# A ninth convolution tap chosen by image half, in a matmul that skips the padded row

## The chip, the cores and the metric

The kernel runs on one core of a Trainium2 chip. The metric is the device time of one execution in microseconds, as the median of three runs. TensorE (PE) multiplies matrices, and its weight loads (PEld) are listed apart from its matmuls; VectorE (DVE), ScalarE (ACT) and GpSimd (POOL) work element by element; SyncE (SP) issues DMAs, as ACT and POOL do too.

## The reference

Four residual layers work on an input x of shape (4, 32, 32, 16): batch, height, width, channels. Each layer normalises x over 8 groups of channels and adds the result of a convolution-like operator. In the first three layers this operator has its own 3x3 kernel for every one of the 1024 output positions (i, j):

```python
first = jnp.einsum('ijpq,bpqc->bijc', M2, inputs)
K = jnp.transpose(G, (2, 3, 4, 0, 1, 5)).reshape(kh, kw, c, h * w * f)
shifted = lax.conv_general_dilated(inputs, K, window_strides=(1, 1), padding='SAME', ...)
shifted = shifted.reshape(b, h, w, h, w, f)
diff = jax.nn.relu(inputs[:, :, :, None, None, :] - shifted)
second = jnp.einsum('ijpq,bpqijc->bijc', W2, diff)
return first - L * second
```

So for each position (i, j) and each filter the whole image is convolved with 9 taps x 16 channels, the result is subtracted from the normalised image, clipped at zero, and summed over the image with the weights W. The fourth layer is a filter in the frequency domain; the change does not touch it. With 'SAME' padding, a tap of the upper row of the 3x3 kernel reads only zeros where it is applied to the image's first row, and a tap of the lower row reads only zeros at the image's last row.

## The kernel before

**Tiling.** Positions are worked on in 128 blocks of 8 positions x 16 filters, which are the 128 columns of the weights. A block and one of the four batches make a group. Its result, 128 x 1024 pixels, lies in two PSUM banks, one for the upper 16 image rows (`half` 0) and one for the lower 16 (`half` 1). The contraction over 9 taps x 16 channels is 144 deep. It is split into three operands (L539 to L548): `ga` with image 0 (four taps, 64 rows, in fp32), `gb` with image 1 (four taps, 64 rows, in fp32) and `gn` with image 2 (the ninth tap, in fp32r). For the ninth tap, weights and pixels are each cut into a rounded high part and a remainder, which gives four products of 16 channels, so again 64 rows. Partitions 0 to 63 of each image serve the upper half and partitions 64 to 127 the lower half, so the matmuls of the two halves use different rows of the array. An fp32 matmul shows in the trace as two passes, each with its own weight load; the fp32r matmul shows as one. VectorE then takes the minimum with zero, multiplies by the weights W and sums, in one instruction (L550), into `acc`.

**Image layout.** Each of the three images is a tile of 128 partitions x 4 (l) x 2 (batch of the pair) x 4 (cc) x 34 values. An image row is 32 values in a field of 34, and one batch's 16 rows are read with the pattern 4 x 4 x 32. The order of taps is one list for both halves, with tap 8 (lower right) as the ninth:

```python
TAPS = [0, 1, 3, 4, 2, 5, 6, 7, 8]
```

**Order of the work.** The order is written out by hand (`manual_schedule`). A layer (`conv_layer`, L499) begins with the first 8 blocks for batches 0 and 1, then the same blocks for batches 2 and 3, goes on through the blocks 8 to 119 for all four batches, and ends with the last 8 blocks for batches 0 and 1 and then for 2 and 3. Each of these part jobs for one pair has 16 groups. Beside them run small steps: G weights are loaded (`load_g`) and prepared (`prepare_g`: POOL subtracts on `ga`, ACT casts `gn`, VectorE subtracts its remainder), W tiles are loaded by SP (`load_w`), and the term with M (`first_term`, L378) is computed.

**The images of layer 0** come from the host (`raw`), through `load_first` (L183) on SP. `first_images` (L196) normalises them in place: VectorE for images 0 and 2 (`first_tap`, `last_tap`), ACT for most of image 1, and POOL clears the pixels that stand for padding (`clear`, L210). The first matmuls wait for this.

**The images of layers 1 and 2** are rebuilt when a pair of batches has ended its layer, while the other pair's 16 groups run: `store_image` (L340) normalises, cuts into high part and remainder (L345, L347), copies edges (L348 on POOL, L349 on ACT), and stores three kinds of rows (whole, high, remainder) to DRAM. `load_image` (L356) then loads each tap's shifted view with 24 DMAs, dealt in turn to SP, ACT and POOL; loads that need an edge copy come last. SP's loads of W stand behind its share of these.

Of the kernel before, what the change touches and what calls it, by code (L numbers as in the profile page):

```python
# [29 lines left out]
F32 = mybir.dt.float32  # L30
F32R = mybir.dt.float32r
AF = mybir.ActivationFunctionType
ALU = mybir.AluOpType
# [4 lines left out]
P = 128  # L38
B, C, S = 4, 16, 32
NBLK = 128  # L40
TAPS = [0, 1, 3, 4, 2, 5, 6, 7, 8]
ROW = 2 * 4 * 34
RUN = ROW - 2
GC = 8
NK = S // 2
NF = S * NK
# [9 lines left out]
def conv_stack_kernel(ctx, tc, x, raw, M, W, first_w, G, h0, coef, cst, dft, idp, idq, out):  # L56
# [31 lines left out]

    ys, ye, img = [], [], []
    for a in range(2):  # L90
        ys.append(const.tile([P, 3, 2, 4, 34], F32, name=f"y{a}"))
        ye.append(const.tile([P, 3, 2, 4, 34], F32, name=f"e{a}"))
        img.append(dram.tile([10, C, 3, ROW], F32, name=f"img{a}"))
    hd = dram.tile([8 + C * HLEN], F32, name="hd")
    fd = dram.tile([P, B, 2, 2, S], F32, name="fd")
    td = dram.tile([NK, 2, S, 2 * P], F32, name="td")
# [78 lines left out]
    def image_tiles(a):  # L175


        ims[a] = [
            imp.tile([P, 4, 2, 4, 34], d, tag=f"im{a}{k}", name=f"im{a}{k}")
            for k, d in enumerate((F32, F32, F32R))  # L180
        ]

    def load_first(a, which, b=slice(0, 2)):  # L183

        if a not in ims:
            image_tiles(a)
            nine[a] = st.tile([P, 4, 2, 4, 34], F32, name=f"nine{a}")
        to = nine[a] if which == 2 else ims[a][which]
        nc.sync.dma_start(
            out=to[:, :, b].rearrange("p l b cc x -> p l (b cc x)"),  # L190
            in_=raw[:, a, which].rearrange("p (l b n) -> p l b n", l=4, b=2)[:, :, b].rearrange(
                "p l b n -> p l (b n)"
            ),
        )

    def first_images():  # L196
# [13 lines left out]
        def clear(which, a, b=slice(0, 2)):  # L210

            top, bottom = (0, 0, slice(0, S)), (3, 3, slice(0, S))
            left, right = ((slice(0, 4), slice(0, 4), slice(x, x + 1)) for x in (0, S - 1))
            parts = {
                0: [(g, g + 16, left) for g in range(0, P, 32)] + [(0, 32, top)],
                1: [(g, g + 32, right) for g in (0, 64)]
                + [(g + 32, g + 48, left) for g in (0, 64)]
                + [(0, 16, top), (96, P, bottom)],
                2: [(0, P, right), (64, P, bottom)],
            }[which]  # L220
            for lo, hi, (l, cc, x) in parts:
                nc.gpsimd.memset(ims[a][which].bitcast(F32)[lo:hi, l, b, cc, x], 0.0)

        def first_tap(b, which=0):
            v = of(ims[b // 2][which], b)
# [1 line left out]

        def last_tap(b):

            v, v8, m = of(nine[b // 2], b), of(ims[b // 2][2], b), neg[:, b : b + 1]  # L230
# [101 lines left out]
    def make_image(a, xt):  # L332
# [4 lines left out]
        yield  # L337
        load_image(a)

    def store_image(a, xt, neg, rstd):  # L340
        split = lambda t: t.rearrange("p b (cc q) -> p b cc q", q=S)
        whole, hi, lo = (ys[a][:, k, :, :, 1:33] for k in range(3))
        normalise(a, xt, neg, rstd)
        y = yc[a]
        nc.vector.tensor_copy(hi.bitcast(F32R), split(y))  # L345
        nc.scalar.copy(whole, split(y))
        nc.vector.tensor_tensor(lo, split(y), hi, ALU.subtract)  # L347
        nc.gpsimd.tensor_copy(ye[a][96:, :, :, 1:, :], ys[a][96:, :, :, :3, :])  # L348
        nc.scalar.copy(ye[a][:32, :, :, :3, :], ys[a][:32, :, :, 1:, :])  # L349
        flat = lambda t: t.rearrange("p k b cc x -> p (k b cc x)")  # L350
        rows = img[a].rearrange("p c k x -> p c (k x)")
        nc.sync.dma_start(out=rows[1:9].rearrange("p c x -> (p c) x"), in_=flat(ys[a]))
        nc.scalar.dma_start(out=rows[0], in_=flat(ye[a][7 * C :]))
        nc.scalar.dma_start(out=rows[9], in_=flat(ye[a][:C]))

    def load_image(a):  # L356
        image_tiles(a)
        taps = [(n // 4, n % 4, 0, TAPS[n]) for n in range(8)]
        taps += [(2, n, 1 + n % 2, 8) for n in range(4)]
        jobs = [(half, *tap) for tap in taps for half in range(2)]  # L360

        jobs.sort(key=lambda job: job[4] // 3 == 2 * job[0])
        for n, (half, k, slot, which, tap) in enumerate(jobs):
            at, p = 64 * half + C * slot, 4 * half + tap // 3
            (nc.sync, nc.scalar, nc.gpsimd)[n % 3].dma_start(  # L365
                out=ims[a][k][at : at + C]
                .bitcast(F32)
                .rearrange("c l b cc x -> c l (b cc x)")[:, :, :RUN],
                in_=img[a][p : p + 4, :, which, tap % 3 : tap % 3 + RUN].rearrange(
                    "l c x -> c l x"  # L370
                ),
            )

    def load_m(mt, layer, pm):
        nc.sync.dma_start(out=mt, in_=M[layer][:, pm])
# [123 lines left out]
    def conv_layer(layer, xt, finish, side=(), also=iter(())):  # L499


        acc = [work.tile([P, 2, NBLK], F32, tag=f"acc{a}", name=f"acc{a}") for a in range(2)]
        xn = xp.tile([P, B, NBLK], F32, tag="x", name="x")
        result = {}

        def beside():
            result["xr"] = yield from first_term(layer, xt)
            yield from side

        beside = beside()  # L510
        last = range(NBLK - GC, NBLK)
        jobs = [(range(GC), (0, 1)), (range(GC), (2, 3))]
        jobs += [(range(blk, blk + GC), range(B)) for blk in range(GC, NBLK - GC, GC)]
        jobs += [(last, (0, 1)), (last, (2, 3))]
        for job, (blks, batches) in enumerate(jobs):
            pairs = job < 2, job >= len(jobs) - 2
            groups = [[blk] for blk in blks]
            if layer == job == 0:

                groups[:2] = [[0, 1]]  # L520
            for group in groups:
                for blk in group:
                    k = blk - blks[0]
                    if any(pairs):

                        if k in ((4, 6) if job != len(jobs) - 2 else (0, 2)):
                            list(load_w())
                    elif k % 2 == 0:
                        list(load_w())
                    if k == (3 if job == 0 else 1):  # L530
                        list(load_g(layer, blk // GC + 1))
                    if job and k == 6:
                        list(prepare_g(layer, blk // GC + 1))
                    if job == len(jobs) - 2:
                        next(also, None)
                for b, blk in ((b, blk) for b in batches for blk in group):
                    wt = wts[64 * layer + blk // 2][:, blk % 2, :]
                    pt = pair_psum()
                    for n, (w, im) in enumerate(zip(gt[layer, blk // GC], ims[b // 2])):  # L539
                        for half in range(2):  # L540
                            rows = slice(64 * half, 64 * half + 64)
                            nc.tensor.matmul(  # L542
                                pt[:, half, :],
                                lhsT=w[rows, blk % GC, :],
                                rhs=im[rows, :, b % 2, :, :S],
                                start=n == 0,
                                stop=n == 2,
                            )  # L548
                    junk = junkp.tile([P, S * S], F32, tag="junk", name="junk")
                    nc.vector.scalar_tensor_tensor(  # L550
                        junk,
                        pt.rearrange("p h m -> p (h m)"),
                        0.0,
                        wt,
                        ALU.min,
                        ALU.mult,
                        accum_out=acc[b // 2][:, b % 2, blk : blk + 1],
                    )
# [525 lines left out]
```

## Time and profile before

The kernel takes 3104.75 us, median of 3 runs (3104.68 to 3104.94). The profile is of one execution:

| | |
|---|---|
| span of the profiled execution | 3103.0 us |
| TensorE clock granted | 1.000 |
| TensorE busy | 3094.0 us, 16268 matmuls |
| weight loads busy | 1618.2 us |
| VectorE busy | 2066.7 us |
| POOL busy | 239.6 us |
| ScalarE busy | 74.2 us |
| DMA | 322.46 MB, mean 104 GB/s |
| `ga`, `gb`, `gn` matmul records of L542 | 6144, 6144, 3072; mean 590, 588, 805 ns |
| VectorE L550 | 1536 of mean 1224 ns |

Matmuls are pipelined: the duration of a record is its time from the queue to its last result, and records overlap. The pace of TensorE is read from the distance between starts. "Issue" as a releaser means that nothing in the profile shows what was waited for.

### The profile page before, as it was taken

To read this page: it belongs to the slowest core of one execution; us is meant where nothing else is said; L and a number is where in the kernel's file an instruction comes from. 1 tells how busy PE (TensorE), PEld (TensorE's weight loads), DVE (VectorE), ACT (ScalarE), POOL (GpSimd) and SP (SyncE) were. 2 spreads that over 40 slices of the span, in tenths; PEclk is the share of its full clock that TensorE was granted. 3 is DMA by queue.
4 is the path that set the end of the run, shared out by engine and by line. 5 is a ranking of instruction groups with operands and counts; after the bars stand their busy time and mean duration, and the time that the engine had idled before them with its cause. 6 is when DMAs were issued, how large, how long until landed. Compare 5 with 4: busy or idle time off the path is not lost.

```text
span 3103.0 us, 39162 instructions
## 1 busy us (share of the span) xinstructions
PE 3094.0 (100%) x16268; PEld 1618.2 (52%) x16268; DVE 2066.7 (67%) x3358; ACT 74.2 (2%) x93; POOL 239.6 (8%) x279
## 2 busy tenths in 40 slices
PE   9999999999999999999999999999999999999999
PEld 7854555555555554544545454555444545445454
DVE  7667666666667765666666666776666666666664
ACT  1000000000000000000000000000000000000000
POOL 1022220000000101000000000010100000000000
PEclk9999999999999999999999999999999999999999
DMA  7353443333332745333333333274644454445422
GB/s 231 102 146 89 108 115 95 89 89 95 102 89 62 158 129 129 89 89 95 102 89 89 95 102 89 62 152 128 144 100 97 100 113 104 97 95 119 95 44 42
DMA packets 71003, 322.46 MB, mean 104 GB/s; under 512 B 10409, under 2 KB 20393, under 8 KB 45481
## 3 DMA queue, kind: packets, MB, share of 16 engines
q1 hardware_dynamic: 60592, 302.24, 39.2%
q10 hardware_dynamic: 6152, 9.99, 1.8%
q0 software_dynamic: 4080, 7.72, 1.2%
q8 instruction: 127, 2.08, 0.3%
q14 instruction: 52, 0.42, 0.1%
HBM read 313.64 MB, written 6.28 MB: 103 GB/s over the span
## 4 chain that ended last, share of the span: by engine, by line
PE 100%; DMA 0%; DVE 0%; issue 0%; ACTq 0%; DVEq 0%; ACT 0%
PE pt L542 97%; PE pt L822 1%; PE pt L402 1%; PE pt L576 0%; DMA ga<-in_G_dram 0%; PE pt L649 0%; DVE junk L550 0%; PE pt L690 0%; PE pt L248 0%; DVE ga L460 0%; PE pt L121 0%; ACTq L81 0%; DVE xo L959 0%; DVE d L150 0%; DVE d L153 0%
## 5 line engine op out<-in xcount | busy, mean ns | idle before, releaser
L550 DVE SCALAR_TENSOR_TENSOR junk<-pt,w 128x1024 f32<-128x1024 f32 x1536 | 1880.6, 1224 | 989.0 <-PE pt L542 971.7
L542 PE MATMUL pt<-im,ga 64*128 64x512 f32 x6144 | 1607.4, 590 | 0.0
L542 PE MATMUL pt<-im,gb 64*128 64x512 f32 x6144 | 1600.6, 588 | 0.0
L542 PE MATMUL pt<-im,gn 64*128 64x512 f32 x3072 | 1276.0, 805 | 0.0
L542 PEld LDWEIGHTS pt<-im,gb 64*128 64x128 f32 x6144 | 636.7, 185 | 682.6 <-issue 672.4
L542 PEld LDWEIGHTS pt<-im,ga 64*128 64x128 f32 x6144 | 626.4, 187 | 409.2 <-DVE junk L550 278.3
L542 PEld LDWEIGHTS pt<-im,gn 64*128 64x128 f32 x3072 | 319.7, 186 | 340.3 <-issue 328.5
L460 POOL TENSOR_TENSOR ga<-ga,cs 128x1024 f32<-128x1024 f32 (+1 forms) x48 | 112.5, 2345 | 2025.8 <-DMA ga<-in_G_dram 2025.0
L550 DVE DVE_READ_ACCUMULATOR junk<-pt,w 128x1 f32 x1536 | 127.6, 83 | 0.0
L468 DVE TENSOR_TENSOR gn<-g,gn 32x1024 fp32r<-32x1024 f32 (+2 forms) x98 | 117.7, 1201 | 2.7 <-ACT gn L464 0.6
L464 ACT CAST gn<-g 128x1024 fp32r<-128x1024 f32 (+2 forms) x49 | 50.4, 1029 | 2256.5 <-PE pt L542 2088.2
L417 POOL DMA_DIRECT2D fd<-ft x48 | 25.3, 533 | 318.2 <-ACT ft L409 307.5
L822 PE MATMUL pt<-t,y 128*32 128x512 f32 (+3 forms) x352 | 23.9, 432 | 0.0
L705 POOL COPY hs<-v 32x512 f32<-32x512 f32 x16 | 17.1, 1072 | 47.2 <-ACT v L699 46.6
L946 DVE TENSOR_TENSOR xo<-xo,both 128x512 f32<-128x512 f32 x2 | 1.4, 692 | 26.7 <-DMA both<-sd 26.7
L822 PEld LDWEIGHTS pt<-t,y 128*32 128x32 f32 x352 | 10.9, 110 | 12.8 <-issue 10.9
L365 POOL DMA_DIRECT2D im<-img x32 | 16.1, 513 | 9.3 <-PE pt L542 6.6
L620 POOL TENSOR_TENSOR H<-H,d 128x256 f32<-128x256 f32 x8 | 6.8, 850 | 93.2 <-DVE d L625 92.9
L822 PE MATMUL pt<-t,yp 128*32 128x512 f32 (+3 forms) x192 | 13.6, 434 | 0.0
L348 POOL COPY e<-y 32x612 f32<-32x612 f32 x4 | 2.8, 692 | 129.4 <-DVE y L347 129.4
L402 PE MATMUL pt<-mt,yt 128*64 128x512 f32 x48 | 11.0, 599 | 0.0
L402 PE MATMUL pt<-w,yt 128*64 128x512 f32 x48 | 10.8, 592 | 0.0
(107 smaller groups left out, 192.5 us busy)
## 6 DMA issues: line engine op xcount, KB each, us to landing
w<-in_W_dram SPq DMA_DIRECT2D x188, 1024.0 KB, 7.5
g<-in_G_dram SPq DMA_DIRECT2D x47, 512.0 KB, 7.8
ga<-in_G_dram SPq DMA_DIRECT2D x47, 512.0 KB, 3.5
gb<-in_G_dram SPq DMA_DIRECT2D x47, 512.0 KB, 5.4
mt<-in_M_dram SPq DMA_DIRECT2D x12, 512.0 KB, 9.6
w<-in_M_dram SPq DMA_DIRECT2D x12, 512.0 KB, 4.1
t<-hd ACTq DMA_DIRECT2D x28, 160.0 KB, 7.8
t<-hd SPq DMA_DIRECT2D x28, 160.0 KB, 8.8
```

The costliest lines, as they stand in the source:

```text
L348: nc.gpsimd.tensor_copy(ye[a][96:, :, :, 1:, :], ys[a][96:, :, :, :3, :])
L365: (nc.sync, nc.scalar, nc.gpsimd)[n % 3].dma_start(out=ims[a][k][at : at + C] .bitcast(F32) .rearrange("c l b cc x -> c l (b cc x)")[:, :, ...
L402: nc.tensor.matmul(pf[64 * h : 64 * h + 64], lhsT=yt[:, k].rearrange("k b c -> k (b c)"), rhs=mt[:, bass.ts(h, 512)], start=(k == 0), stop ...
L417: nc.gpsimd.dma_start(out=fv[h, cc, b], in_=ft[at : at + C, cc])
L460: engine.tensor_tensor(gv, gv, mid.unsqueeze(1).to_broadcast([P, gv.shape[1], C]), ALU.subtract)
L464: nc.scalar.copy(gn, g9)
L468: nc.vector.tensor_tensor(lo, g9[r : r + 32], lo.bitcast(F32), ALU.subtract)
L542: nc.tensor.matmul(pt[:, half, :], lhsT=w[rows, blk % GC, :], rhs=im[rows, :, b % 2, :, :S], start=n == 0, stop=n == 2,)
L550: nc.vector.scalar_tensor_tensor(junk, pt.rearrange("p h m -> p (h m)"), 0.0, wt, ALU.min, ALU.mult, accum_out=acc[b // 2][:, b % 2, blk : ...
L620: mul = lambda o, u, w: nc.gpsimd.tensor_tensor(o, u, w, ALU.mult)
L705: nc.gpsimd.tensor_copy(hs[quarter[u], :, bass.ts(c, 8)], v[quarter[c], bass.ts(u, 8)].rearrange("q p m -> q m p"),)
L822: nc.tensor.matmul(rows.rearrange("n (j r) -> n j r", j=C)[:, :, 8 * cc :], lhsT=y(cc).rearrange("p q b -> p (q b)"), rhs=ts[k][q][:, :, : ...
```

## The change

The ninth tap is now chosen by image half. For the upper half it is tap 2 (upper right), for the lower half tap 8 (lower right); tap 8 takes the place of tap 2 among the other eight taps of the upper half. So in each half the ninth tap reads only padding in one image row: the first row in the upper half, the last row in the lower half. Its matmul leaves this row out, and so has 480 columns in place of 512. Image 2 is laid out anew: 2 (batch) x 4 (l) x 4 (cc) x 32, so that one batch's 16 rows are one run of 512 values. In DRAM the high parts and the remainders are stored in the same packed form, shifted by one pixel (both ninth taps look one pixel to the right), and a load of image 2 becomes two DMAs, one for each batch of the pair. The host arranges `raw` and the weights G to match.

```diff
-TAPS = [0, 1, 3, 4, 2, 5, 6, 7, 8]
+TAPS = [0, 1, 3, 4, 8, 5, 6, 7, 2], [0, 1, 3, 4, 2, 5, 6, 7, 8]
+NINE = 2 * 4 * 32
...
-            imp.tile([P, 4, 2, 4, 34], d, tag=f"im{a}{k}", name=f"im{a}{k}")
-            for k, d in enumerate((F32, F32, F32R))
+            imp.tile([P, *shape], d, tag=f"im{a}{k}", name=f"im{a}{k}")
+            for k, (d, shape) in enumerate(
+                ((F32, (4, 2, 4, 34)), (F32, (4, 2, 4, 34)), (F32R, (2, 4, 4, S)))
+            )
...
+        if which == 2:
+            nc.sync.dma_start(
+                out=nine[a][:, b].rearrange("p b l cc x -> p (b l cc x)"),
+                in_=src[:, b.start * 2 * NINE : b.stop * 2 * NINE],
+            )
+            return
...
-                + [(0, 16, top), (96, P, bottom)],
-                2: [(0, P, right), (64, P, bottom)],
+                + [(96, P, bottom)],
+                2: [(0, P, right)],
...
-        nc.vector.tensor_copy(hi.bitcast(F32R), split(y))
-        nc.scalar.copy(whole, split(y))
-        nc.vector.tensor_tensor(lo, split(y), hi, ALU.subtract)
-        nc.gpsimd.tensor_copy(ye[a][96:, :, :, 1:, :], ys[a][96:, :, :, :3, :])
-        nc.scalar.copy(ye[a][:32, :, :, :3, :], ys[a][:32, :, :, 1:, :])
+        hi, lo = hi[..., : S - 1], lo[..., : S - 1]
+        nc.vector.tensor_copy(hi.bitcast(F32R), y[..., 1:])
+        nc.scalar.copy(whole[..., 1:33], y)
+        nc.vector.tensor_tensor(lo, y[..., 1:], hi, ALU.subtract)
+        for e, v in zip(in_rows(ye[a]), in_rows(ys[a])):
+            nc.gpsimd.tensor_copy(e[96:, :, 1:, :], v[96:, :, :3, :])
+            nc.scalar.copy(e[:32, :, :3, :], v[:32, :, 1:, :])
...
-        taps = [(n // 4, n % 4, 0, TAPS[n]) for n in range(8)]
+        taps = [(n // 4, n % 4, 0, n) for n in range(8)]
         taps += [(2, n, 1 + n % 2, 8) for n in range(4)]
-        jobs = [(half, *tap) for tap in taps for half in range(2)]
+        jobs = [(half, *tap, TAPS[half][n]) for *tap, n in taps for half in range(2)]
...
+            if which:
+                moves = [
+                    (to[:, b].rearrange("c l cc x -> c l (cc x)"), src[:, :, bass.ts(b, NINE // 2)])
+                    for b in range(2)
+                ]
+            else:
+                moves = [(to.rearrange("c l b cc x -> c l (b cc x)")[:, :, :size], src)]
+            for out, src in moves:
+                (nc.sync, nc.scalar, nc.gpsimd)[n % 3].dma_start(
+                    out=out, in_=src.rearrange("l c x -> c l x")
+                )
...
+                            px = (slice(S, None), slice(0, -S))[half] if n == 2 else slice(None)
+                            if n == 2:
+                                rhs = im[rows, b % 2].rearrange("p l cc x -> p (l cc x)")[:, px]
+                            else:
+                                rhs = im[rows, :, b % 2, :, :S]
                             nc.tensor.matmul(
-                                pt[:, half, :],
+                                pt[:, half, px],
                                 lhsT=w[rows, blk % GC, :],
-                                rhs=im[rows, :, b % 2, :, :S],
+                                rhs=rhs,
                                 start=n == 0,
                                 stop=n == 2,
                             )
...
-        taps = g[:, P:], g[:, :64], g[:, 64:P]
-        arrays[f"G{i}"] = np.stack([np.tile(t, (1, P // t.shape[1], 1)) for t in taps], 1)
+        parts = slice(8 * C, None), slice(0, 4 * C), slice(4 * C, 8 * C)
+        taps = [[np.tile(t[:, part], (1, 1 if n else 4, 1)) for t in g] for n, part in enumerate(parts)]
+        arrays[f"G{i}"] = np.stack([np.concatenate(t, 1) for t in taps], 1)
```

More of the change, by code (lines that the diff above doesn't have):

```diff
@@ L90, in conv_stack_kernel @@
     for a in range(2):
-        ys.append(const.tile([P, 3, 2, 4, 34], F32, name=f"y{a}"))
-        ye.append(const.tile([P, 3, 2, 4, 34], F32, name=f"e{a}"))
-        img.append(dram.tile([10, C, 3, ROW], F32, name=f"img{a}"))
+        ys.append(const.tile([P, ROW + 2 * NINE], F32, name=f"y{a}"))
+        ye.append(const.tile([P, ROW + 2 * NINE], F32, name=f"e{a}"))
+        img.append(dram.tile([10, C, ROW + 2 * NINE], F32, name=f"img{a}"))
     hd = dram.tile([8 + C * HLEN], F32, name="hd")
@@ L186, in load_first @@
             image_tiles(a)
-            nine[a] = st.tile([P, 4, 2, 4, 34], F32, name=f"nine{a}")
-        to = nine[a] if which == 2 else ims[a][which]
+            nine[a] = st.tile([P, 2, 4, 4, S], F32, name=f"nine{a}")
+        src = raw[:, a, 4 * ROW * which :][:, : 4 * (NINE if which == 2 else ROW)]
+        if which == 2:
[4 more added lines that the diff above has]
+            return
+        to = ims[a][which]
         nc.sync.dma_start(
             out=to[:, :, b].rearrange("p l b cc x -> p l (b cc x)"),
-            in_=raw[:, a, which].rearrange("p (l b n) -> p l b n", l=4, b=2)[:, :, b].rearrange(
+            in_=src.rearrange("p (l b n) -> p l b n", l=4, b=2)[:, :, b].rearrange(
                 "p l b n -> p l (b n)"
@@ L212, in clear @@
             top, bottom = (0, 0, slice(0, S)), (3, 3, slice(0, S))
+            t = ims[a][which].bitcast(F32)
+            if which == 2:
+                t = t.rearrange("p b l cc x -> p l b cc x")
             left, right = ((slice(0, 4), slice(0, 4), slice(x, x + 1)) for x in (0, S - 1))
@@ L217, in clear @@
                 + [(g + 32, g + 48, left) for g in (0, 64)]
-                + [(0, 16, top), (96, P, bottom)],
-                2: [(0, P, right), (64, P, bottom)],
+                + [(96, P, bottom)],
+                2: [(0, P, right)],
             }[which]
             for lo, hi, (l, cc, x) in parts:
-                nc.gpsimd.memset(ims[a][which].bitcast(F32)[lo:hi, l, b, cc, x], 0.0)
+                nc.gpsimd.memset(t[lo:hi, l, b, cc, x], 0.0)
         def first_tap(b, which=0):
@@ L228, in last_tap @@
         def last_tap(b):
-            v, v8, m = of(nine[b // 2], b), of(ims[b // 2][2], b), neg[:, b : b + 1]
+            v, v8 = (
+                t[:, b % 2].rearrange("p l cc x -> p (l cc x)") for t in (nine[b // 2], ims[b // 2][2])
+            )
+            m = neg[:, b : b + 1]
             nc.vector.tensor_scalar(v8, v, m, rstd[:, b : b + 1], ALU.add, ALU.mult)
@@ L338, in make_image, with in_kinds, in_rows @@
         load_image(a)
+    def in_kinds(t):
+        whole = t[:, :ROW].rearrange("p (b cc x) -> p b cc x", b=2, cc=4)
+        pieces = t[:, ROW:].rearrange("p (k b cc x) -> p k b cc x", k=2, b=2, cc=4)
+        return whole, pieces[:, 0], pieces[:, 1]
+    def in_rows(t):
+        return (
+            t[:, :ROW].rearrange("p (b cc x) -> p b cc x", b=2, cc=4),
+            t[:, ROW:].rearrange("p (kb cc x) -> p kb cc x", kb=4, cc=4),
+        )
     def store_image(a, xt, neg, rstd):
-        split = lambda t: t.rearrange("p b (cc q) -> p b cc q", q=S)
@@ L342, in store_image @@
-        whole, hi, lo = (ys[a][:, k, :, :, 1:33] for k in range(3))
         normalise(a, xt, neg, rstd)
-        y = yc[a]
-        nc.vector.tensor_copy(hi.bitcast(F32R), split(y))
-        nc.scalar.copy(whole, split(y))
-        nc.vector.tensor_tensor(lo, split(y), hi, ALU.subtract)
-        nc.gpsimd.tensor_copy(ye[a][96:, :, :, 1:, :], ys[a][96:, :, :, :3, :])
-        nc.scalar.copy(ye[a][:32, :, :, :3, :], ys[a][:32, :, :, 1:, :])
-        flat = lambda t: t.rearrange("p k b cc x -> p (k b cc x)")
@@ L351, in store_image @@
[L351 to L354, printed above, removed]
+        y = yc[a].rearrange("p b (cc q) -> p b cc q", q=S)
+        whole, hi, lo = in_kinds(ys[a])
+        hi, lo = hi[..., : S - 1], lo[..., : S - 1]
+        nc.vector.tensor_copy(hi.bitcast(F32R), y[..., 1:])
+        nc.scalar.copy(whole[..., 1:33], y)
@@ L356, in load_image @@
+        nc.vector.tensor_tensor(lo, y[..., 1:], hi, ALU.subtract)
+        for e, v in zip(in_rows(ye[a]), in_rows(ys[a])):
+            nc.gpsimd.tensor_copy(e[96:, :, 1:, :], v[96:, :, :3, :])
+            nc.scalar.copy(e[:32, :, :3, :], v[:32, :, 1:, :])
+        rows = img[a]
+        nc.sync.dma_start(out=rows[1:9].rearrange("p c x -> (p c) x"), in_=ys[a])
+        nc.scalar.dma_start(out=rows[0], in_=ye[a][7 * C :])
+        nc.scalar.dma_start(out=rows[9], in_=ye[a][:C])
     def load_image(a):
@@ L364, in load_image @@
             at, p = 64 * half + C * slot, 4 * half + tap // 3
[L365 to L372, printed above, removed]
+            start, size = (ROW + NINE * (which - 1), NINE) if which else (tap % 3, RUN)
+            src = img[a][p : p + 4, :, start : start + size]
+            to = ims[a][k][at : at + C].bitcast(F32)
+            if which:
[8 more added lines that the diff above has]
+                    out=out, in_=src.rearrange("l c x -> c l x")
+                )
     def load_m(mt, layer, pm):
@@ L1029 @@
     raw = np.zeros((2, 4, C, 2, 3, 4, 2, 4, 34), x.dtype)
-    for n in range(12):
-        dy, dx = divmod(TAPS[min(n, 8)], 3)
-        v = around[:, dy : dy + S, dx : dx + S].reshape(2, 2, 4, 2, 4, S, C)
-        raw[:, n % 4, :, :, n // 4, :, :, :, :S] = v.transpose(3, 6, 0, 4, 1, 2, 5)
+    for half in range(2):
+        for n in range(12):
+            dy, dx = divmod(TAPS[half][min(n, 8)], 3)
+            v = around[:, dy : dy + S, dx : dx + S].reshape(2, 2, 4, 2, 4, S, C)[:, :, :, half]
+            raw[half, n % 4, :, :, n // 4, :, :, :, :S] = v.transpose(5, 0, 3, 1, 2, 4)
+    raw = raw.reshape(P, 2, 3, 4, 2, 4, 34)
+    raw = [raw[:, :, 0], raw[:, :, 1], raw[:, :, 2, ..., :S].transpose(0, 1, 3, 2, 4, 5)]
+    raw = np.concatenate([v.reshape(P, 2, -1) for v in raw], 2)
     arrays = {
         "x": x.reshape(B, 4, 8, S, C).transpose(2, 4, 0, 1, 3).reshape(P, B, NBLK),
-        "raw": raw.reshape(P, 2, 3, -1),
+        "raw": raw,
     }
@@ L1050 @@
             arrays["first_w"] = np.repeat(w.reshape(64, 8, 2 * S * S)[:4], C, axis=1)
-        g = g[:, :, :, TAPS].transpose(0, 2, 3, 4, 1, 5).reshape(NBLK // GC, GC, 9 * C, P)
-        g = g.transpose(0, 2, 1, 3).reshape(NBLK // GC, 9 * C, GC * P)
-        taps = g[:, P:], g[:, :64], g[:, 64:P]
-        arrays[f"G{i}"] = np.stack([np.tile(t, (1, P // t.shape[1], 1)) for t in taps], 1)
+        g = [
+            g[:, :, :, taps].transpose(0, 2, 3, 4, 1, 5).reshape(NBLK // GC, GC, 9 * C, P)
+            for taps in TAPS
+        ]
+        g = [t.transpose(0, 2, 1, 3).reshape(NBLK // GC, 9 * C, GC * P) for t in g]
+        parts = slice(8 * C, None), slice(0, 4 * C), slice(4 * C, 8 * C)
+        taps = [[np.tile(t[:, part], (1, 1 if n else 4, 1)) for t in g] for n, part in enumerate(parts)]
+        arrays[f"G{i}"] = np.stack([np.concatenate(t, 1) for t in taps], 1)
     pairs = lambda t: t.reshape(-1, 4, 4, C).transpose(0, 1, 3, 2).reshape(-1, 2 * P)
```

## The prediction

> **What bounds the kernel now.** I read the page first (busy shares, then the chain that ended last), then that chain in order of time, then single groups in the timeline. From the page:
>
> ```profile
> span 3103.0 us, 39162 instructions
> ...
> PE 3094.0 (100%) x16268; PEld 1618.2 (52%) x16268; DVE 2066.7 (67%) x3358; ACT 74.2 (2%) x93; POOL 239.6 (8%) x279
> ...
> PE 100%; DMA 0%; DVE 0%; issue 0%; ACTq 0%; DVEq 0%; ACT 0%
> ```
>
> TensorE holds the whole chain. In order of time that chain has three long stretches of L542; the longest shows what one group (one block, one batch: 4 matmul records on `ga`, 4 on `gb`, 2 on `gn`) costs:
>
> ```profile
> 1201.40 813.02 PE pt L542 x4140
> ```
>
> 4140 records are 414 groups, so a group takes 813.02 / 414 = 1.964 us, and 3 layers x 128 blocks x 4 batches = 1536 groups are 3016 us of the 3103. Now one group, from the timeline (start, duration, engine):
>
> ```profile
> 1500.71 1.03 PE L542 MATMUL pt<-im,gb 64*128 64x512 f32 x4
> 1500.72 0.20 PEld L542 LDWEIGHTS pt<-im,gb 64*128 64x128 f32 x2 [0.23 <-issue]
> 1501.15 0.20 PEld L542 LDWEIGHTS pt<-im,gn 64*128 64x128 f32 x2 [0.23 <-issue]
> 1501.17 0.82 PE L542 MATMUL pt<-im,gn 64*128 64x512 f32 x2
> ...
> 1501.58 0.45 PEld L542 LDWEIGHTS pt<-im,ga 64*128 64x128 f32 x4 [0.23 <-DVE junk L550]
> 1501.82 1.03 PE L542 MATMUL pt<-im,ga 64*128 64x512 f32 x4
> 1502.03 1.22 DVE L550 SCALAR_TENSOR_TENSOR junk<-pt,w 128x1024 f32<-128x1024 f32 x1 [0.73 <-PE pt L542]
> ```
>
> The start written for a `gn` matmul is that of its queueing. The weight loads tell the true rhythm: each begins as the matmul before it starts to stream (1500.72, 1501.15, 1501.58). So the two fp32 passes of `gb` are 0.43 us apart (both image halves run side by side, each on 64 rows), and the fp32r matmul of `gn` streams from 1501.58 to 1501.82. With four fp32 passes of 0.43 (1.72), `gn` has 1.964 - 1.72 = 0.244 us of each group.
>
> **What the skill says of it.** "TensorE: Matmul & The Clock Gate", section "Back-to-back issue gap": a warm stream spaces matmuls by N / 2.4 + 2.5 ns. With 1024 cycles for an fp32 pass of 512 columns that is 429 ns, and the trace has 0.43 us. With 512 cycles for the single fp32r pass it is 216 ns, and the trace has 244: 28 ns more. What these 28 ns are decides this forecast, so I looked for them in two places.
>
> Are they the next weight load? After the last group before the first term, the next load comes late, because it waits:
>
> ```profile
> 176.27 0.59 PE L542 MATMUL pt<-im,gb 64*128 64x512 f32 x1
> 176.30 0.81 PE L542 MATMUL pt<-im,gn 64*128 64x512 f32 x1
> ...
> 177.03 0.20 PEld L402 LDWEIGHTS pt<-mt,yt 128*64 128x64 f32 x4 [0.57 <-DVE junk L550]
> ...
> 177.14 1.22 DVE L550 SCALAR_TENSOR_TENSOR junk<-pt,w 128x1024 f32<-128x1024 f32 x1 [0.73 <-PE pt L542]
> ```
>
> There nothing loads while `gn` streams, and VectorE still starts 177.14 - 176.27 = 0.87 us after the second `gb` pass; in the group above it is 1502.03 - 1501.15 = 0.88. The same skill page (section "Step-by-step: what each phase is for") says that loading weights steals no read bandwidth from the running matmul; this agrees. And loads alone can follow faster: at 1001.34 a matmul of 16 columns (L121) starts, its successor's second pass begins at 1001.88, so the first began 0.43 earlier, at 1001.45: 0.11 us after L121. So 0.24 is no floor from loading.
>
> Then it is how the operand is read. "SBUF — State Buffer", section "Door 1" (its note on cachelines), says that SBUF has lines of 16 bytes and that an access which crosses to a new line pays a penalty. The image of `gn` lies in 16 rows of 32 values with a pitch of 34, so 136 bytes: every second row starts in the middle of a line, and the stream breaks 16 times. 28 ns / 16 = 1.7 ns, four array cycles per row. In the fp32 passes, at two cycles a column, the same rows cost nothing visible (0.43 us is the formula for unbroken data). No wide fp32r matmul on packed rows is in this trace, so the attribution to rows is not shown by it.
>
> **The change, part by part**
>
> 1. *480 columns for 512 in the `gn` matmuls.* 32 / 2.4 = 13.3 ns in each group (the two halves run side by side): 1536 x 13.3 ns = 20.5 us, on the path. Order and count of matmuls stay.
> 2. *Packed rows under the same matmul.* Bounds: 0 (the 28 ns belong to fp32r itself) and 28 ns x 1536 = 43 us. A loss I exclude: one run of 480 values has no more lines or steps than 16 rows. I take the whole 28, because both the load and the neighbour are excluded above and four cycles a row is a natural size. `gn` would then take 480 / 2.4 + 2.5 = 202.5 ns, well over the 0.11 us that a load needs.
> 3. *First image.* The third image loads as 256 KB in runs of 2 KB for 272 KB; three VectorE operations of 0.56, 0.56 and 0.78 us shrink by 32 of 544 elements (0.03 to 0.05 us each); the 64x32 memset (198 ns, POOL) and the 16x32 one fall away. Only the first two groups feel it: `gn` waits for POOL at 13.18 and at 13.64, the later one for the memset that goes. At most 0.5 us; I take 0.3.
> 4. *Image rebuilds, two after layer 0 and two after layer 1.* Each of the 8 third-image loads becomes two, of 64 rows x 512 B where one had 64 rows x 1080 B: 32 loads for 24; SP gets 10, ACT 11, POOL 11, where each had 8. POOL's issues take 0.51 us, so 1.5 us more there; ACT and SP 0.31, so up to 0.9, plus waits for landings. Two smaller edge copies replace one of 0.70 on POOL and on ACT: 0.2 us more. All this is under the other pair's 16 groups (31 us). How much cover: for the second pair ACT issues the last load at 1052.2; the median landing is 5.4 us later, 1057.6; its first group starts at 1060.69 and reads the third image 1.7 us after that. Cover is 3.1 us for the first two images, 4.8 for the third. All third-image loads now come last in the order, so the first two images are complete earlier. DMA is near full there (99% of the engines), but bytes fall: 2 x 512 for 1080 in a row. A row of 512 B costs between 512/1080 of one of 1080 and as much; in the second case 32 loads take a third longer than the 12.5 us of now, 4.2 more, still inside 4.8. W loads stand behind these on SP; SP waited 1933 us for buffers of W in the run, so it has room. I take 0; without cover it is some us in all.
> 5. *Weights of the ninth tap* differ by half, in the same bytes and instructions: 0.
>
> Sum: 20.5 + 43 + 0.3 = 64 us; 3103.0 - 64 = 3039 of span. The median of the runs (3104.75) is 1.75 above the profiled span, so **3041 us**.
>
> Nothing else takes over: VectorE needs 1.22 + 0.08 us in a group of 1.92, and 2067 us in all.
>
> **The rivals.** *(B) The 28 ns are fp32r's own.* For it: no packed wide fp32r matmul is here to compare. Against: the L121 matmuls, also fp32r, show no fixed extra of that size (0.17 us for 16 columns, where the fp32 passes exceed their stream by 0.16). Then only columns count: 3104.75 - 20.8 = 3084. *(C) Only the half lines at odd rows count*, 8 of them at 1.7 ns, half of the 28: 3084 - 21 = 3063. *(D) Slower: the rebuilds come late.* 64 packets per load in 32 loads, with the semaphores of earlier landings between them, could make TensorE wait at each of four rebuilds. It decides when each wait passes 20.8 / 4 = 5.2 us in case B (16 in case A), that is, when the last landing comes 5.2 + 4.8 = 10 us later than now, a rebuild of 22 us where it takes 12.5; above the 4.2 that a third more packets give. At 8 us of wait each, in case B: 3116. *(E) The matmul is not shortened at all*, its cost being set by something other than columns: against it, the fp32 passes follow the column formula exactly; about 3104.
>
> **How the numbers follow.** A 0.58, B 0.27, C 0.10, D 0.03, E 0.02. The range holds A, C and B with 3 to 5 us around the outer ones (rebuild waits above, fuller removal of the 5 ns by which a group's first pass exceeds the others below): 3036 to 3087. A measurement here tells 0.2% (6 us); A, B and C are all beyond it: faster 0.95, same 0.02, slower 0.03.
>
> **What would show it.** Step 1 and 2: the long stretch of layer 1 at 1.922 us a group (A), 1.950 (B), 1.937 (C), and a `ga` matmul 0.20 us after the weight load that stands ahead of it, for 0.24. Step 3: the second `gn` load of the first groups ahead of 13.6. Step 4: no idle TensorE where the rebuilt images are first read, near the 512th and 1024th groups. Wrong would be: groups at 1.95, which sinks step 2; or the right group time with missing microseconds at the rebuilds, which sinks step 4.

## The result, and the profile after

The changed kernel takes 3061.06 us (median of 4 runs, 3061.04 to 3061.51), the kernel before 3104.72 us: a ratio of 0.9859, 95% interval 0.9845 to 0.9873, or 43.7 us less. That lies inside the range that was forecast (3036 to 3087), which held three of the theories and so does not tell them apart. It is 20 us above the number that was named (3041) and 2 us from the value of rival C (3063).

From the page of the changed kernel:

```profile
span 3059.2 us, 39208 instructions
...
PE 3049.9 (100%) x16268; PEld 2080.0 (68%) x16268; DVE 2066.2 (68%) x3358; ACT 74.8 (2%) x97; POOL 245.9 (8%) x288
...
PE 99%; DVE 0%; DMA 0%; issue 0%; ACT 0%; POOL 0%; ACTq 0%; DVEq 0%
...
L583 PE MATMUL pt<-im,gn 64*128 64x480 f32 x3072 | 1574.2, 778 | 0.0
```

TensorE still holds the chain, with as many matmuls as before, and VectorE's busy time has not moved. The `gn` records now have 480 columns. Weight loads are busy for 2080 us where they had 1618, without being more or longer: the page counts stretches in which at least one load runs, and the two image halves, which ran in step for most of the kernel before, now run out of step, so that their loads overlap less. The same holds for the busy sums of the matmul groups.

The chain in order of time, same stretch as before (from the end of layer 1's first term, 414 groups; some records of it fell out of this chain's count):

```profile
1183.98 800.86 PE pt L583 x3862
```

800.86 / 414 = 1.934 us a group, where 813.02 us gave 1.964. One group in the timeline of the changed kernel (start, duration, engine), and the `ga` matmuls of a group 103 groups later:

```profile
1301.31 0.28 PEld L583 LDWEIGHTS pt<-im,gn 64*128 64x128 f32 x2
...
1301.74 0.50 PEld L583 LDWEIGHTS pt<-im,ga 64*128 64x128 f32 x4
1301.95 1.12 PE L583 MATMUL pt<-im,ga 64*128 64x512 f32 x4
1302.26 1.23 DVE L591 SCALAR_TENSOR_TENSOR junk<-pt,w 128x1024 f32<-128x1024 f32 x1 [0.70 <-PE pt L583]
...
1501.08 1.29 PE L583 MATMUL pt<-im,ga 64*128 64x512 f32 x4
```

From the weight load of the next `ga`, which marks the start of `gn`'s stream, to that `ga` matmul it is now 0.21 us (0.24 before).

The two `ga` lines show that the two halves have different paces. The four `ga` matmuls of a group (two of each half) lie in one line, which is 1.03 us long where the halves run in step. It is 1.12 us long at 1301.95 and 1.29 at 1501.08, so one half has fallen behind by 0.17 us more. The half ahead takes (1501.08 - 1301.95) / 103 = 1.9333 us a group, the half behind (199.13 + 0.17) / 103 = 1.9350. The chain above starts with the halves in step and ends with the half ahead, so it reads a little short; the half behind sets the time. With four fp32 passes of 0.429, `gn` has 1.935 - 1.717 = 0.218 us to itself in the half behind, where it had 0.246. That is 15.5 ns more than the 480 / 2.4 + 2.5 = 202.5 ns of the forecast (14 ns in the half ahead). 1536 groups at 1.9633 - 1.9350 = 28.3 ns less are 43.5 us, and the span fell by 43.8; the first groups make up the rest.

The start of the kernel changed as told, by a little:

```profile
10.66 1.13 PE L583 MATMUL pt<-im,ga 64*128 64x512 f32 x4
...
12.53 1.50 POOL L235 MEMSET im<- 128x16 f32 x4 [0.49 <-DVE im L251]
...
13.00 0.19 PEld L583 LDWEIGHTS pt<-im,gn 64*128 64x128 f32 x2 [0.61 <-POOL im L235]
...
13.33 1.02 PE L583 MATMUL pt<-im,ga 64*128 64x512 f32 x4
```

Both `gn` loads start at 13.0 (13.18 and 13.64 before), and the second group at 13.33 in place of 13.65: 0.32 us. The first group began 0.9 us earlier (10.66 for 11.52), but then waited for the other images, so this was worth nothing more.

### The profile page after: what moved, and what is told of

It is laid out like the page before. It is cut to its first block, busy times and chain, and to the rows that moved or that the text cites. A ratio compares the mean times of both kernels' runs of the same rounds, so it can differ in the third digit from the quotient of the medians.

```text
span 3059.2 us, 39208 instructions
## 1 busy us (share of the span) xinstructions
PE 3049.9 (100%) x16268; PEld 2080.0 (68%) x16268; DVE 2066.2 (68%) x3358; ACT 74.8 (2%) x97; POOL 245.9 (8%) x288
## 4 chain that ended last, share of the span: by engine, by line
PE 99%; DVE 0%; DMA 0%; issue 0%; ACT 0%; POOL 0%; ACTq 0%; DVEq 0%
PE pt L583 97%; PE pt L863 1%; PE pt L437 1%; DMA g<-in_G_dram 0%; DVE junk L591 0%; PE pt L690 0%; PE pt L731 0%; PE pt L617 0%; POOL im L235 0%; DVE im L239 0%; DVE gn L503 0%; ACT gn L499 0%; DVE st L142 0%; ACT L781 0%; DVE x L606 0%
## 5 line engine op out<-in xcount | busy, mean ns | idle before, releaser
L583 PE MATMUL pt<-im,ga 64*128 64x512 f32 x6144 | 1941.8, 588 | 0.1
L583 PE MATMUL pt<-im,gb 64*128 64x512 f32 x6144 | 1940.7, 588 | 0.0
L583 PE MATMUL pt<-im,gn 64*128 64x480 f32 x3072 | 1574.2, 778 | 0.0
L583 PEld LDWEIGHTS pt<-im,gb 64*128 64x128 f32 x6144 | 916.6, 186 | 418.0 <-issue 294.3
L583 PEld LDWEIGHTS pt<-im,ga 64*128 64x128 f32 x6144 | 919.6, 185 | 174.4 <-issue 68.8
L583 PEld LDWEIGHTS pt<-im,gn 64*128 64x128 f32 x3072 | 509.2, 186 | 334.9 <-issue 270.0
L863 PE MATMUL pt<-t,y 128*32 128x512 f32 (+3 forms) x352 | 23.9, 432 | 0.0
L405 POOL DMA_DIRECT2D im<-img x44 | 22.3, 513 | 17.2 <-DMA img<-y 9.8
```

Of the source, the lines that this page charges most:

```text
L405: (nc.sync, nc.scalar, nc.gpsimd)[n % 3].dma_start(out=out, in_=src.rearrange("l c x -> c l x"))
L583: nc.tensor.matmul(pt[:, half, px], lhsT=w[rows, blk % GC, :], rhs=rhs, start=n == 0, stop=n == 2,)
L863: nc.tensor.matmul(rows.rearrange("n (j r) -> n j r", j=C)[:, :, 8 * cc :], lhsT=y(cc).rearrange("p q b -> p (q b)"), rhs=ts[k][q][:, :, : ...
```

## The experiments

In what follows the group time is the mean distance between the last `ga` matmuls of 400 successive groups of layer 1 (the groups 600 to 1000), read from the trace of each run; that is the pace of the half behind. The kernel before has 1.9633 us by this reading, the changed one 1.9350. The halves run in step where 384 or 512 columns are used and in experiment 11. Elsewhere the half ahead reads less, as long as its lead still grows; the expectations were written with such readings (1.934 us for the changed kernel).

**1. The packed rows alone.** The matmul runs over all 512 columns of packed rows.

```diff
-                2: [(0, P, right)],
+                2: [(0, P, right), (0, 64, top), (64, P, bottom)],
...
-                            px = (slice(S, None), slice(0, -S))[half] if n == 2 else slice(None)
+                            px = slice(None)
```

> The packed rows alone: the ninth tap runs over all 512 columns again, the padded row included (its clearing on POOL is restored). Two parts theory (columns 13.3 ns a group, packing about 15): groups of 1.948 us, 3061 + 20.5 = 3081.5 us. Columns alone (packing is worth nothing, and the 29 ns a group came from the 32 columns): groups of 1.964 us, 3105 us. Packing alone (the columns are worth nothing): groups of 1.934 us, 3061 us.

Measured: 3080.01 us, ratio 0.9921 (0.9906 to 0.9935), groups of 1.9467 us. From its chain in order of time:

```profile
1191.95 806.12 PE pt L583 x4138
```

That is 1.947 us a group for the 414 groups. Both theories of a single cause fall. Packing is worth 3104.72 - 3080.01 = 24.7 us (16.1 ns a group; 16.6 by the group times), the 32 columns 3080.01 - 3061.06 = 19.0 us (12.3 ns a group; 11.7 by the group times).

**2. The 480 columns alone, rows 34 apart.**

```diff
-NINE = 2 * 4 * 32
+XP = 34
+NINE = 2 * 4 * XP
...
-                                rhs = im[rows, b % 2].rearrange("p l cc x -> p (l cc x)")[:, px]
+                                rhs = im[rows, b % 2].rearrange("p l cc x -> p (l cc) x")
+                                rhs = rhs[:, (slice(1, None), slice(0, -1))[half], :S]
```

> The 480 columns alone: image 2 keeps the order of the changed kernel, but its rows lie 34 values apart, as before. Two parts theory: packing is taken away, groups of 1.949 us, 3061 + 23 = 3084 us. Columns alone: groups of 1.934 us, 3061 us. Packing alone: groups of 1.964 us, 3105 us.

Measured: 3076.86 us, ratio 0.9910 (0.9895 to 0.9925), groups of 1.9450 us. Two parts again, but packing is worth only 15.8 us or 10.0 ns a group here, where experiment 1 gave 16. Experiment 4 takes this up. In the profiled execution TensorE also waited for a load of image 2, at the second pair's rebuild after layer 1, and those groups came 0.8 us late:

```profile
2019.94 6.79 DMA im<-img
2026.73 0.14 issue
2026.86 160.40 PE pt L585 x740
```

This is the wait that the prediction's rival D feared, at one rebuild of four.

**3. The same with rows 36 apart.** `XP = 36`; every row starts at a multiple of 16 bytes.

> As with rows 34 values apart, but 36: the rows are still broken 14 times, and each starts at a multiple of 16 bytes. Half lines theory (rows that start in the middle of a 16-byte line cost): as packed, groups of 1.934 us, 3061 us. Row steps theory (every break of the run costs about 1 ns, wherever the row starts): as with 34, groups of 1.949 us, 3084 us.

Measured: 3063.87 us, ratio 0.9869 (0.9852 to 0.9885), groups of 1.9367 us, near the packed rows' 1.9350. The rows are still broken, and the breaks cost little; rows that begin in the middle of a 16-byte line cost 1.9450 - 1.9367 = 8.3 ns a group. Matmuls of the two kernels in the timeline, pitch 34 first; the distance from one `ga` to the next is a group:

```profile
1500.99 1.28 PE L585 MATMUL pt<-im,ga 64*128 64x512 f32 x4
...
1502.93 1.28 PE L585 MATMUL pt<-im,ga 64*128 64x512 f32 x4
...
1504.87 1.28 PE L585 MATMUL pt<-im,ga 64*128 64x512 f32 x4
```

and pitch 36:

```profile
1500.51 1.12 PE L585 MATMUL pt<-im,ga 64*128 64x512 f32 x3
...
1501.47 0.59 PE L585 MATMUL pt<-im,ga 64*128 64x512 f32 x1
...
1502.44 1.12 PE L585 MATMUL pt<-im,ga 64*128 64x512 f32 x3
...
1504.38 1.13 PE L585 MATMUL pt<-im,ga 64*128 64x512 f32 x3
```

So it is half lines in the main, and not row steps: 1.94 us against 1.935 for the half ahead within the timeline's 10 ns, and 13.0 us between the two medians. The line at 1501.47 is the last pass of the half behind. It comes 0.96 us after the group's first, where halves in step have 0.43; the lag was 0.02 us after the layer's first term and reaches 1.29. This half takes 1.9367 us a group, the other 1.9333. The 1.7 ns over the packed rows' 1.9350 make 2.6 us in 1536 groups, nearly all of the 2.8 us by which this kernel stays behind the packed one. The last matmul issued in a group is the lower half's, and its record carries the signal to VectorE; by this mark the half behind is the lower one here and in experiment 2, and the upper one in the changed kernel. So the breaks cost the lower half 3.3 ns (1.9333 to 1.9367) and the upper half nothing. Why is open.

**4. All 512 columns, rows 34 apart, one row step.** As experiment 2, without leaving out a row. The kernel before has the same pitch, but its 16 rows are read with two steps (4 x 4), because the batch lies between them.

> All 512 columns and rows 34 values apart, as in the kernel before, but with the batch outside of the row index, so that the 16 rows have one step. Packed rows at 512 columns took groups of 1.947 us, the kernel before 1.9635; at 480 columns a pitch of 34 cost 10 ns over packed rows. Half lines theory: 8 rows start in the middle of a line, as at 480 columns in the upper half, so 10 ns: groups of 1.957 us, 3080 + 15.5 = 3096 us, and the other 6.5 ns of the kernel before belong to its pattern of 4 x 4 rows with two steps. Without that pattern's part: groups of 1.9635 us, 3105 us; then what the unpacked rows cost goes with the last row too.

Measured: 3100.95 us, ratio 0.9987 (0.9981 to 0.9994), groups of 1.9600 us. Its chain, the same stretch:

```profile
1199.84 811.64 PE pt L585 x4140
```

This falls between the two expectations. Half lines cost 1.9600 - 1.9467 = 13.3 ns with 16 rows (8 of them begin in mid-line: 1.7 ns each), and the other 3.3 ns of the kernel before come with its own layout (its two steps were not taken apart further). With 480 columns (experiment 2) 7 of the lower half's 15 rows begin in mid-line, and it takes 1.9450 - 1.9333 = 11.7 ns more than with packed rows, which is 1.7 ns each again. In the upper half it is 8 rows, and 1.9433 - 1.9350 = 8.3 ns; why not 13.3 stays open.

**5. 384 columns.** Four rows are left out in place of one.

```diff
-                            px = (slice(S, None), slice(0, -S))[half] if n == 2 else slice(None)
+                            px = (slice(4 * S, None), slice(0, -4 * S))[half] if n == 2 else slice(None)
```

> The ninth tap leaves out four image rows of each half in place of one: 96 columns of its product are not computed. In the changed kernel a ninth-tap matmul has 0.216 us to itself, 13 ns over 480 columns at one a cycle. Fixed extra theory (the 13 ns come with each matmul, the columns go at one a cycle): 96 x 0.417 = 40 ns less, groups of 1.894 us, 3061 - 61 = 3000 us. Slow columns theory (fp32r takes 0.216 / 480 = 0.45 ns a column): 43 ns less, groups of 1.891 us, 2995 us. Floor theory (0.216 us is set by the next weight load or another wait): groups of 1.934 us, 3061 us.

Measured: 2997.28 us, between the two first expectations; groups of 1.8933 us, with the halves in step. Its chain, the same stretch:

```profile
1159.33 784.04 PE pt L583 x4140
```

784.04 / 414 = 1.894 us. No floor is in sight. Against the 512 packed columns of experiment 1 it is 53.4 ns less for 128 columns, 0.417 ns a column, so the columns go at one a cycle and not at 0.45 ns. `gn` has 1.8933 - 1.717 = 0.176 us, which is 14 ns more than 384 / 2.4 + 2.5 = 162.5; with 512 columns it is 14 ns too. Against the changed kernel it is 41.7 ns for 96 columns, because one half of that kernel has 15.5 ns in place of 14 (experiment 9).

**6. The `gn` matmul twice in a row.** This puts a price on one more fp32r matmul.

```diff
-                    for n, (w, im) in enumerate(zip(gt[layer, blk // GC], ims[b // 2])):
+                    trio = [*enumerate(zip(gt[layer, blk // GC], ims[b // 2]))]
+                    for at, (n, (w, im)) in enumerate([*trio, trio[2]]):
...
-                                stop=n == 2,
+                                stop=at == 3,
```

> The ninth-tap matmul of 480 packed columns is issued twice in a row in every group, so its product is added twice. In the changed kernel it has 0.216 to 0.217 us to itself where 480 columns at one a cycle need 0.2025. Switch theory (the extra 14 ns come from the change from fp32 to fp32r and back): the second one costs 0.2025 us, 1536 x 0.2025 = 311 us, 3372 us in all, groups of 2.136 us. Own theory (each fp32r matmul carries the 14 ns): 0.2165 us, 333 us more, 3394 us, groups of 2.150 us.

Measured: 3396.25 us, 335.2 us more than the changed kernel, 218 ns for each second matmul. Its chain, the same stretch:

```profile
1314.36 891.39 PE pt L584 x4213
```

891.39 / 414 = 2.153 us a group. The extra comes again, with an fp32r matmul right before it. The switch theory falls.

**7. Every second group in turned order, 512 columns.** A second way to ask the same.

```diff
-                    for n, (w, im) in enumerate(zip(gt[layer, blk // GC], ims[b // 2])):
+                    order = list(enumerate(zip(gt[layer, blk // GC], ims[b // 2])))
+                    flip[0] = not flip[0]
+                    for at, (n, (w, im)) in enumerate(order[::-1] if flip[0] else order):
...
-                                start=n == 0,
-                                stop=n == 2,
+                                start=at == 0,
+                                stop=at == 2,
```

> Packed rows, all 512 columns, and every second group takes its three operands in the turned order, so that two ninth-tap matmuls follow each other and changes between fp32 and fp32r are halved. To be compared with the packed 512 columns in plain order, 3080 us. Switch theory: half of 14 ns a group less, 3080 - 11 = 3069 us. Own theory: 3080 us.

Measured: 3080.15 us, the 3080.01 of the plain order. Its chain has the very figure of experiment 1 for the stretch:

```profile
1192.10 806.12 PE pt L586 x4139
```

**8. The same, with 480 columns where the ninth tap comes last.**

> As before, every second group turned, with 480 columns where the ninth tap comes last and 512 where it comes first and so begins the sum: 496 in the mean, 6.5 ns a group more than the changed kernel, 10 us. Switch theory: 3061 + 10 - 11 = 3060 us. Own theory: 3071 us.

Measured: 3072.94 us, ratio 0.9898 (0.9883 to 0.9912). The own theory again, within 2 us.

**9. The ninth tap in the upper half alone.**

```diff
+                            if n == 2 and half:
+                                continue
...
-                                stop=n == 2,
+                                stop=n == 2 - half,
```

> The ninth tap is left out in the lower half, so one fp32r matmul stands alone in each group. Sharing theory (the 14 ns come from two fp32r streams side by side): 0.2025 us for it, groups of 1.920 us, 3061 - 21 = 3040 us. Own theory: groups of 1.934 us, 3061 us.

Measured: 3061.05 us, groups of 1.9350 us: exactly the changed kernel. Two fp32r streams side by side do not hinder each other, and the lower half's matmul costs nothing beside the upper one's. So here too the half behind in the changed kernel, with 1.9350 us and 15.5 ns of extra, is the upper one; the lower one needs 1.9333. Why the upper half, which leaves out its first row, takes 1.7 ns more was not tested. The difference is absent with 384 columns and in experiment 11.

**10. The same places read as bf16.**

```diff
+                            lhs = w[rows, blk % GC, :]
+                            if n == 2:
+                                rhs = im[rows, b % 2].rearrange("p l cc x -> p (l cc x)")
+                                rhs = rhs.bitcast(mybir.dt.bfloat16).rearrange("p (n k) -> p n k", k=2)[:, px, 1]
+                                lhs = lhs.bitcast(mybir.dt.bfloat16).rearrange("p (n k) -> p n k", k=2)[:, :, 1]
...
-                                lhsT=w[rows, blk % GC, :],
+                                lhsT=lhs,
```

> The ninth tap reads the upper 16 bits of the same values in the same places as bf16, weights too, so its product has fewer digits; columns, places and order stay. If the 14 ns belong to the type fp32r: 0.2025 us, groups of 1.920 us, 3040 us. If every matmul of one cycle a column has them here: groups of 1.934 us, 3061 us.

Measured: 3050.95 us, groups of 1.9283 us. Between the two: in the half that sets the time 6.7 ns of the 15.5 go with the type, 8.8 stay.

**11. High parts and remainders held as bf16, packed.** Pixels, weights and the stored rows in bf16 tiles.

```diff
-                ((F32, (4, 2, 4, 34)), (F32, (4, 2, 4, 34)), (F32R, (2, 4, 4, S)))
+                ((F32, (4, 2, 4, 34)), (F32, (4, 2, 4, 34)), (BF16, (2, 4, 4, S)))
...
-            gt[at] = *gr[at][:2], gs.tile([P, GC, P], F32R, tag="gn", name="gn")
+            gt[at] = *gr[at][:2], gs.tile([P, GC, P], BF16, tag="gn", name="gn")
...
-        pieces = t[:, ROW:].rearrange("p (k b cc x) -> p k b cc x", k=2, b=2, cc=4)
+        pieces = t[:, ROW:].bitcast(BF16).rearrange("p (k b cc x) -> p k b cc x", k=2, b=2, cc=4)
...
-                nc.vector.tensor_tensor(lo, g9[r : r + 32], lo.bitcast(F32), ALU.subtract)
+                nc.vector.tensor_tensor(lo, g9[r : r + 32], lo, ALU.subtract)
```

> The high parts and remainders of the ninth tap, of pixels and of weights, are held as bf16 in packed tiles, so the product has some 16 bits in place of more; the rest is the changed kernel. Reading the upper halves of 4-byte words as bf16 gave groups of 1.927 us for 1.934, half of the 14 ns. Bytes theory (the rest goes with the 4 bytes that each column still spans): 480 columns in 0.2025 us, groups of 1.920 us, 3040 us. Fixed theory (the rest comes with a matmul of one cycle a column, whatever it reads): groups of 1.927 us, 3051 us. The rebuild's loads of image 2 come in runs of 256 bytes for 512, which may add some us after the layers.

Measured: 3037.20 us, ratio to the kernel before 0.9782 (0.9766 to 0.9799), groups of 1.9192 us. Chain and one group:

```profile
1175.10 794.74 PE pt L587 x4140
```

```profile
1502.68 0.10 PEld L587 LDWEIGHTS <-gn 64*128 64x128 bf16 x2 [0.24 <-issue]
...
1503.11 0.37 PE L587 MATMUL pt<-im,gn 64*128 64x480 bf16 x2
1503.11 0.40 PEld L587 LDWEIGHTS pt<-im,ga 64*128 64x128 f32 x4 [0.33 <-DVE junk L595]
1503.31 1.02 PE L587 MATMUL pt<-im,ga 64*128 64x512 f32 x4
```

794.74 / 414 = 1.920 us, and `gn` has 1.919 - 1.717 = 0.202 us: 480 columns at one a cycle, with nothing left over. Here the `gn` record starts where its stream starts, and the next `ga` follows 0.20 us later. The bytes theory holds: what experiment 10 left goes when the values lie 2 bytes apart, so the extra of the changed kernel belongs in part to the type fp32r and in part to the 4 bytes that each value spans. Among the kernels that compute the whole sum this is the fastest, 23.9 us below the changed one, at some 16 bits for the ninth tap's operands. The weight loads became shorter too (93 ns in the mean for 186 in fp32r), in experiment 10 as well as here, and pixels and weights changed type together; that the pixels are what counts is argued from the load's cover (0.3 us between its end and the start of its matmul here, 0.2 us in the kernel before), not shown.

## Why the prediction came out as it did

*What bounds the kernel.* Right. TensorE set the time in every run, but for the 0.8 us in experiment 2, and the reading of the group (true starts from the weight loads, 244 ns for `gn`, 28 of them unexplained) held but for rounding: 1.964 us became 1.935 by shortening just that piece. The prediction took four passes at 0.43 us; at its own 429 ns the unexplained part is 1963.3 - 1717 - 216 = 30 ns, not 28. Its formula for the spacing held as well. The Trainium skill ("TensorE: Matmul & The Clock Gate", section "Back-to-back issue gap") gives it for the gap of an isolated matmul and names a lower figure, about 131 ns for 512 columns, for a sustained stream; in the sustained stream of each half here an fp32 pass took 429 ns and the bf16 matmul of experiment 11 202, both by the formula.

*Step 1, 480 columns for 512.* Right: forecast 20.5 us, measured 19.0 alone; experiment 5 gives 0.417 ns a column over 128 columns. What is missing goes with the 1.7 ns that the upper half takes more at 480 columns.

*Step 2, the packed rows.* This step failed in size. It gave the rows all 28 ns, "because both the load and the neighbour are excluded above and four cycles a row is a natural size", 43 us; packing was worth 24.7 (experiment 1). The 28 ns (30 by the closer sum) had two causes of about equal size: the layout of the rows (13.3 ns for the rows that start in mid-line at 512 columns, experiments 3 and 4, and 3.3 ns that go with the old order of batch and rows) and the type and 4-byte spacing of the operands (14 ns, experiments 10 and 11). Excluding two suspects left more than one. The step's 1.7 ns, "four array cycles per row", fits every second row only.

*Rival B* was put down with too weak a witness. The argument was that a 16-column fp32r matmul shows no such extra. It shows none, but a matmul of 384 columns does: if the two kinds of matmul can be compared, the extra is there in full somewhere between 16 and 384 columns, so a short record could not speak for a long one.

*Rival C* named the half lines and a price of 1.7 ns for each of 8 rows. The mechanism and the price are what the runs showed for the rows; it had a chance of 0.10 for want of a reason to prefer it. That its total comes within 2 us is luck in part: it left out the old layout's 3.3 ns and counted 13.5 ns for the columns, where the group times give 11.7. The rest of the 28 ns, which it did not explain, is where rival B was right. The Trainium skill's note on 16-byte lines ("SBUF — State Buffer", section "Door 1") speaks of crossing to a new line, and would have spoken for C rather than for A: a row pitch that is a multiple of 16 bytes crosses no additional line, whatever its breaks. Experiment 3 agrees with that note but for 3.3 ns in the lower half. The note gives no price; the 1.7 ns for each such row are from experiment 4.

*Step 3* was right to a few hundredths: 0.32 us for 0.3. *Step 4*, the rebuilds: no wait of TensorE for them is in the chain. ACT's share of the second pair's loads after layer 0 is eleven, as told:

```profile
1030.02 9.37 ACTq L405 DMA_DIRECT2D im<-img  x11
...
1044.99 1.25 PE L583 MATMUL pt<-im,ga 64*128 64x512 f32 x4
```

The last of them is issued by 1039.4, SP's last one at 1041.2, and the pair's groups start at 1044.99. The last three loads, from 1039.1 on, have no landing in the trace; the landings that it has end at 1042.7. At none of the four rebuilds do TensorE's groups come late, so rival D did not come here. It was near: experiment 2, with rows 34 apart in the stored form too, lost 0.8 us to it at one rebuild.

*The sum.* 64 us forecast, 43.7 measured: 18 us short in step 2 and 1.5 in step 1. Nothing of size was lost outside the groups, where the half behind is read: 28.3 ns in 1536 groups are 43.5 us.

## What to carry to other kernels

When a stage's pace exceeds a formula by a few per cent, split the excess by one run for each suspect, or give each suspect its share in the forecast; ruling out two does not hand the rest to a third. For fp32r operands that stream at one column a cycle, try packed rows or a row pitch that is a multiple of 16 bytes: packing was worth 13 ns a matmul of 512 columns, a pitch of 36 for 34 values 8 ns at 480. Ask whether a 4-byte operand type is needed there: the split into two bf16 parts, with fewer bits, ran at the full rate where the split into fp32r did not. And where two streams share a stage, read the pace of the one behind.

## What the runs showed that I had not expected

- An fp32r matmul of 384, 480 or 512 packed columns takes some 14 ns longer than its columns at one a cycle and 2.5 ns; bf16 of 480 packed columns takes 0.202 us, bf16 in steps of 4 bytes about 0.211.
- Row breaks as such are nearly free in fp32r: with a pitch of 36 they cost nothing in the upper half and 3.3 ns a group in the lower one. Rows that begin in mid-line cost more, 13.3 ns at 512 columns.
- The two halves, on separate rows of the array, keep their own pace for a while. In the changed kernel one runs at 1.9333 us a group until it is 0.43 us ahead, then both at 1.9350; with a pitch of 36 the lead grows to 1.29 us. The lead has no effect on the half behind, and leaving the lower half's `gn` out altogether gained nothing.
